# Group statistics by a DRAM round trip and an indirect DMA in place of two small matrix products, in a masked attention kernel

## The chip, the cores and the metric

The kernel runs on one core of one Trainium2 chip. The metric is the device time of one execution in microseconds (us). A core has five engines that work side by side, each through its own list of instructions in order: TensorE (PE in the profile; its weight loads are PEld), VectorE (DVE), ScalarE (ACT), GpSimd (POOL) and SyncE (SP), which here only issues DMAs. GpSimd issues DMAs too. They meet through semaphores.

## The reference

The input x is 32 images of 256 channels and 32 x 32 positions, all float32. Each image is normalised in 32 groups of 8 channels; query, key and value are 1x1 convolutions of the result; eight heads of width 32 attend with a strict causal mask over the 1024 positions; the attention's output is added to x.

```python
def _gn(v, G=32, eps=1e-5):
    g = v.reshape(B_, G, C_ // G, H_, W_)
    m = jnp.mean(g, axis=(2, 3, 4), keepdims=True)
    s = jnp.var(g, axis=(2, 3, 4), keepdims=True)
    return ((g - m) / jnp.sqrt(s + eps)).reshape(v.shape)
...
q = jnp.einsum('oc,bcs->bos', q_w, xf) + q_b[None, :, None]
kv = jnp.einsum('oc,bcs->bos', kv_w, xf) + kv_b[None, :, None]
...
scores = jnp.einsum('bhqd,bhkd->bhqk', q, k) / jnp.sqrt(jnp.asarray(dk, x.dtype))
scores = jnp.where(mask == 0, jnp.asarray(-10000.0, x.dtype), scores)
attn = jnp.where(mask == 0, 0.0, jax.nn.softmax(scores, axis=-1))
out = jnp.einsum('bhqk,bhkd->bhqd', attn, v)
...
x = x + _L0_conv_ref(_gn(x), ...)
```

## The kernel before, in words

**Tiles.** An image lies as 128 partitions x 2 channel groups x 1024 positions. Channels are on partitions, so a group of the normalisation is 8 neighbouring partitions. Heads 0 to 3 belong to the first half of the channels (g = 0), heads 4 to 7 to the second.

**Visits.** The attention of an image is cut into N = 12 visits, six for each g (`VISITS`, lines 583 to 590). A visit computes the transposed scores of four heads for a set of key blocks and queries (`scores`, line 348): a long part of up to 512 columns and a short part, on TensorE's row groups of 32, so that heads 0 and 1 and heads 2 and 3 run beside each other. Scores go to three PSUM tiles of two banks, which every visit uses again; ScalarE takes the exponentials into SBUF (`e`, line 397, twice; `eh`, line 393); on diagonal blocks GpSimd masks them (`mask`, line 329; four of the six visits, `PAIRS`). One visit later TensorE multiplies them by the values (`values`, line 412), and VectorE adds the exponentials of several key blocks together (`add_keys`, line 434), from which the softmax sums are made: folded by accumulating DMAs (`fold`, line 449), stacked (`stack`, line 455), inverted and spread over DRAM. `finish` (line 539) multiplies the attention's numerators by the inverses and adds bias and x: one multiplication (L544), two L547, on VectorE, and a DMA out. It is put two images later: for image b at visits 1, 1, 2 and 4 of image b + 2 (`FINISH`, line 656).

**Normalisation.** `norm_channels` (line 179) takes mean and variance of each channel on VectorE (bn_stats over two halves of 512, then bn_aggr). `norm_mean` (line 187) averages the means over 8 partitions by a small matrix product with the constant `avg` (tile `pm`); ScalarE writes it negated (L195). `norm_deviation` (line 198) makes variance plus squared deviation on VectorE (L205 to L207), `norm_variance` (line 210) averages that by a second product (tile `pv`), ScalarE adds eps (L219). `norm_rstd` (line 221) takes the power -0.5 and the shift on GpSimd (L227, L229). `norm_apply` (line 231) normalises on ScalarE (L244), two instructions for each of four quarters. Then TensorE projects (`project_qk`, `project_v`; `pp` and `ppv`).

**Order.** The order on each engine is written out by hand (`tc.manual_schedule`): every engine issues in the order of the program's text. The main loop (line 750) runs over i, visit v of image b: scores of visit i, what is listed in `at` for i, values of visit i - 1, what is listed in `between`, `add_keys` of visit i - 1, what is listed in `after`. Within a list the order is that of appending; the loop at line 706 appends, image by image, `prepare(b)` and then `finish(b)`, so the `finish` of an older image stands ahead of the `prepare` of a newer one. `PREPARE` (line 652) says at which visit, counted from the image's first, each step of the normalisation is put: -12 and -11 the two channel halves, -9 mean and deviation (in `between`), -8 variance and rstd, -7, -6, -5 and -3 the four quarters of `norm_apply`. Image 1 has its own list (line 705), image 0 is prepared ahead of the loop, with `keep_busy` products meanwhile. `ALIGN` puts 24 drains on VectorE and 64 waits on GpSimd at the start.

## Time and profile before

| | |
|---|---|
| median of 3 runs | 1793.47 us (1793.45 to 1793.51) |
| the profiled execution's own time | 1793.44 us |
| its span in the profile | 1791.7 us |
| mean granted TensorE clock | 0.999 |
| ScalarE waiting for `pm`, for `pv` | 25.9 us in 30 waits, 13.4 us in 30 |
| bn_stats, 512 elements | 679 ns, 128 times |
| bn_aggr, 12 elements | 209 ns, 64 times |
| `pow` on GpSimd (L227) | 716 to 1387 ns, median 1150 |
| `shift` on GpSimd (L229) | 308 to 1619 ns, median 313 |
| SP's DMA of the inverses, 32 KB, issue to landing | 3.2 us |
| GpSimd's DMA of 512 KB, issue to landing | 5.4 to 5.9 us |

How to read it: the span is one execution, and what lies around it is 1.7 us. A row of the timeline gives start and duration in us, engine, source line, operation, and `out<-in` by the program's names; "x2" means that two equal instructions stand merged in one row. What stands in brackets at the end is the engine's idle time ahead of the row and what ended it. TensorE's matrix products overlap, so the durations of one engine's rows can't be added; the distance of their starts can. Image n of 0 to 31 has visits 12n to 12n + 11; image 16's visit 0 starts at 900.21, 1 at 904.78, 2 at 909.33, 3 at 913.53, 4 at 918.56, 5 at 923.16, 6 at 927.79, 7 at 932.36, 8 at 936.92, 9 at 941.12 (first product of the scores), and in it the statistics of image 17 are made.

### The profile page before, as it was taken

Reading aid. Unit: us, or ns where it says so; the run is one execution under the profiler, and the core shown is the slowest. Engines: PE = TensorE matmul, PEld = TensorE weight load, DVE = VectorE, ACT = ScalarE, POOL = GpSimd, SP = SyncE. Lnnn points to the kernel's source line nnn. Section 1 sums busy time; section 2 is a strip of 40 time slices with the busy share of each in tenths; the row PEclk is TensorE's granted clock in tenths of the full one; section 3 lists DMA queues with packets and bytes.
Section 4 is the critical chain, followed back from the end, with each engine's and each line's share of the span. In section 5 each row is a group of like instructions: output and inputs, shape, how many; then the busy total and the mean of one; then the engine's idle time right before and its main releaser. Section 6 shows DMA issues by size and latency. Waiting matters only on the chain.

```text
span 1791.7 us, 81825 instructions
## 1 busy us (share of the span) xinstructions
PE 1784.4 (100%) x37036; PEld 948.2 (53%) x37036; DVE 1673.4 (93%) x1826; ACT 1456.4 (81%) x1990; POOL 881.3 (49%) x903
## 2 busy tenths in 40 slices
PE   9999999999999999999999999999999999999998
PEld 5555555555555555555555555555555555555554
DVE  4689999999999999999999999999999999999998
ACT  6888878888788888788887888878888878888785
POOL 2345544554545555445554455454555544555452
PEclk9999999999999999999999999999999999999999
DMA  2566766767667766766676676767776667666664
GB/s 70 105 115 137 134 134 129 147 135 143 127 126 149 140 138 134 135 139 138 139 135 131 129 150 132 145 125 128 149 141 135 136 134 138 139 139 137 132 107 106
DMA packets 86818, 236.77 MB, mean 132 GB/s; under 512 B 21312, under 2 KB 22336, under 8 KB 70592
## 3 DMA queue, kind: packets, MB, share of 16 engines
q0 software_dynamic: 15872, 97.53, 40.1%
q1 hardware_dynamic: 70448, 133.89, 25.5%
q8 instruction: 290, 4.75, 1.1%
q14 instruction: 64, 0.52, 0.1%
q10 hardware_dynamic: 144, 0.07, 0.0%
HBM read 66.85 MB, written 34.57 MB: 57 GB/s over the span
## 4 chain that ended last, share of the span: by engine, by line
PE 99%; ACT 0%; DVE 0%; issue 0%; POOL 0%; POOLq 0%
PE sT L311 31%; PE acc L422 28%; PE pp L169 26%; PE ppv L169 13%; PE pd L474 1%; PE busy L155 0%; ACT e L397 0%; PE pv L169 0%; PE pm L169 0%; PE wt L148 0%; DVE rb_last L547 0%; ACT eh L393 0%; DVE rb_last L534 0%; DVE turned L531 0%; DVE acc L544 0%
## 5 line engine op out<-in xcount | busy, mean ns | idle before, releaser
L339 POOL TENSOR_SCALAR_AFFINE_SELECT diagonal<-eh 128x512 f32<-128x512 f32 x512 | 632.5, 1256 | 841.5 <-ACT eh L393 840.9
L397 ACT ACTIVATE e<-sT 128x1024 f32<-128x1024 f32 x768 | 744.4, 1022 | 250.3 <-PE sT L311 225.9
L440 DVE TENSOR_TENSOR e<-e,e 128x1024 f32<-128x1024 f32 x314 | 574.2, 1829 | 24.5 <-ACT v L275 3.2
L311 PE MATMUL sT<-q,k 32*64 32x128 f32 (+2 forms) x18432 | 578.4, 372 | 0.1
L311 PEld LDWEIGHTS sT<-q,k 32*64 32x64 f32 x18432 | 394.8, 131 | 188.4 <-PE sT L311 69.6
L169 PE MATMUL pp<-xn,wT 128*32 128x512 f32 x4096 | 492.2, 598 | 0.0
L422 PE MATMUL acc<-e,v 128*32 128x512 f32 (+3 forms) x4608 | 401.0, 450 | 0.0
L393 ACT ACTIVATE eh<-sT 128x768 f32<-128x768 f32 (+1 forms) x384 | 341.7, 890 | 0.0
L422 PEld LDWEIGHTS acc<-e,v 128*32 128x32 f32 x4608 | 149.2, 110 | 261.5 <-issue 238.9
L169 PE MATMUL ppv<-wT,xn 128*32 128x256 f32 x4096 | 247.5, 382 | 0.0
L440 DVE TENSOR_TENSOR diagonal<-diagonal,e 128x1536 f32<-128x1536 f32 x126 | 195.0, 1548 | 16.8 <-PE acc L422 9.2
L169 PEld LDWEIGHTS pp<-xn,wT 128*32 128x32 f32 x4096 | 107.0, 109 | 195.7 <-issue 163.7
L440 DVE TENSOR_TENSOR e<-e,eh 128x1024 f32<-128x1024 f32 x126 | 164.2, 1303 | 6.5
L422 PEld LDWEIGHTS acc<-diagonal,v 128*32 128x32 f32 x4096 | 121.1, 110 | 87.6 <-issue 76.0
L440 DVE TENSOR_TENSOR e<-e,diagonal 128x2048 f32<-128x2048 f32 x63 | 144.2, 2289 | 19.8 <-POOL diagonal L339 19.8
L169 PEld LDWEIGHTS ppv<-wT,xn 128*32 128x32 f32 x4096 | 120.1, 109 | 79.7 <-issue 7.0
L422 PE MATMUL acc<-diagonal,v 128*32 128x128 f32 x4096 | 158.7, 273 | 0.0
L244 ACT ACTIVATE xn<-x,shift,rstd 128x256 f32<-128x256 f32 x248 | 136.8, 608 | 0.6 <-POOL shift L229 0.6
L544 DVE TENSOR_TENSOR num<-num,rb 128x512 f32<-128x512 f32 x124 | 123.3, 994 | 0.2 <-DMA rb<-inverses 0.2
L453 POOL DMA_DIRECT2D e<-e x124 | 103.3, 833 | 38.2 <-issue 38.2
L547 DVE SCALAR_TENSOR_TENSOR rb<-num,v_bias_col,x 128x256 f32<-128x256 f32 x248 | 117.5, 515 | 4.4
L453 POOL DMA_DIRECT2D diagonal<-diagonal x124 | 104.1, 839 | 4.8 <-issue 4.8
(84 smaller groups left out, 984.4 us busy)
## 6 DMA issues: line engine op xcount, KB each, us to landing
x<-in_x_dram SPq DMA_DIRECT2D x124, 256.0 KB, 3.7
diagonal<-diagonal POOLq DMA_DIRECT2D x62, 512.0 KB, 5.4
e<-e POOLq DMA_DIRECT2D x62, 512.0 KB, 5.9
rb<-inverses SPq DMA_DIRECT2D x124, 256.0 KB, 3.9
out_dram<-rb SPq DMA_DIRECT2D x124, 256.0 KB, 4.9
diagonal<-diagonal POOLq DMA_DIRECT2D x62, 256.0 KB, 4.6
folded<-diagonal SPq DMA_DIRECT2D x62, 256.0 KB, 5.1
e<-e POOLq DMA_DIRECT2D x62, 256.0 KB, 5.0
```

The source lines that it names most:

```text
L169: nc.tensor.matmul(out[part], lhsT=lhsT[:, part], rhs=rhs, start=start, stop=stop, skip_group_check=True)
L244: nc.scalar.activation(to, of, AF.Identity, bias=live["shift", b][:, g : g + 1], scale=rstd)
L311: return nc.tensor.matmul(bank[c : c + KEYS, cols], lhsT=live["k", b, g][rows, kb * P + c : kb * P + c + KEYS], rhs=live["q", b, g][rows, ...
L339: nc.gpsimd.affine_select(out=square[:, :, place + s * P : place + (s + 1) * P], in_=raw[:, :, (1 - s) * KEYS : (3 - s) * KEYS], pattern=[ ...
L393: exp = nc.scalar.activation(eh.rearrange("p (n bank) q -> p bank n q", n=2)[:, :, :, :narrow], short[:, :, :, :narrow], AF.Exp)
L397: nc.scalar.activation(e[:, 2 * a : 2 * a + 2, :wide], pairs[a][:, :, :wide], AF.Exp)
L422: nc.tensor.matmul(acc[HD * j : HD * (j + 1), of], lhsT=live["v", b][:, kb, h * HD : (h + 1) * HD], rhs=e[:, j, :], start=first, stop=last ...
L440: nc.vector.tensor_add(to, to, tile_of(b, g, at))
L453: nc.gpsimd.dma_start(out=total[:rows], in_=total[rows : 2 * rows], accum_op=ALU.add)
L474: nc.tensor.matmul(pd[HD * j : HD * (j + 1), of], lhsT=pick, rhs=e[:, j, :], start=start, stop=stop, skip_group_check=True,)
L544: nc.vector.tensor_mul(num, num, rb)
L547: nc.vector.scalar_tensor_tensor(blocks(rb, s), blocks(num, s, (start + s) % 2 == 1), v_bias_col[:, g : g + 1], blocks(xt[:, g, cols], s), ...
```

## The change

For every image but the first, the average over 8 partitions no longer runs on TensorE. `norm_channels` keeps the raw statistics of both halves (24 numbers per channel). `norm_gather` writes them to DRAM by SP; `norm_spread` reads them back by an indirect DMA of GpSimd, row `partition / 8` of an array of 16 rows, so that each partition gets the 8 x 24 numbers of its group; `norm_groups` runs bn_aggr over them, 96 numbers per call. `norm_signs`, on VectorE, makes the negated mean and the variance plus eps, which ScalarE did. `norm_rstd` and `norm_apply` stay as they are.

`PREPARE` is now -12, -11 (channels), -10, -10 (gather, spread), -9 (groups), -8 (signs), -8 (rstd), -7, -6, -5, -3 (apply), all in `after`; the second `norm_channels` is put at the head of its list, ahead of `finish`, the rest is appended. `between` is gone.

In visits 3 and 4 (`SPLIT`) the long part of heads 0 and 1 is issued as 128 and 384 columns, the 128 between the short products of heads 2 and 3. At visits 2 and 8 (`EVEN`) TensorE waits once more for a semaphore count ahead of the values. `ALIGN` becomes 22 drains on VectorE, no waits on GpSimd, 16 drains on SP. The last image is left out of the split, and of the added waits.

```diff
--- before.py
+++ after.py
@@ -89,6 +89,10 @@
     in_range = const.tile([P, ROW], F32, name="in_range")
     nc.gpsimd.memset(in_range, 1.0)
     inv_last = const.tile([P, 4, HALF // HD], F32, name="inv_last")
+    place = const.tile([P, 1], mybir.dt.uint32, name="place")
+    nc.gpsimd.iota(place, pattern=[[0, 1]], base=0, channel_multiplier=1)
+    group_of = const.tile([P, 1], mybir.dt.uint32, name="group_of")
+    nc.vector.tensor_scalar(group_of, place, 3, None, ALU.logical_shift_right)
     eps = const.tile([P, 1], F32, name="eps")
     nc.gpsimd.memset(eps, 1e-5)
 
@@ -179,52 +183,68 @@
         def norm_channels(b, g):
             if g == 0:
                 live["mv", b] = small.tile([P, NG, 2], F32, tag="mv", name=f"mv_{b}")
-            st = small.tile([P, NH, 6], F32, tag="st", name=f"st_{b}_{g}")
+                live["st", b] = small.tile([P, NG, NH * 6], F32, tag="st", bufs=1, name=f"st_{b}")
+            st = live["st", b][:, g, :].rearrange("p (c s) -> p c s", c=NH)
             for c in range(NH):
                 nc.vector.bn_stats(st[:, c, :], live["x", b][:, g, c * HALF : (c + 1) * HALF])
-            nc.vector.bn_aggr(live["mv", b][:, g, :], st)
+            if b == 0:
+                nc.vector.bn_aggr(live["mv", b][:, g, :], st)
+
+        def norm_gather(b):
+
+
+            n = NH * 6
+            each = live["each", b] = dram.tile([P, NG * n], F32, tag="st", name=f"each_{b}")
+            nc.sync.dma_start(out=each, in_=live.pop(("st", b)).rearrange("p g s -> p (g s)"))
+
+        def norm_spread(b):
+
+            n = NH * 6
+            eight = small.tile([P, HALF], F32, tag="turned", bufs=1, name=f"eight_{b}")[:, : CPG * NG * n]
+            live["eight", b] = eight.rearrange("p (c g s) -> p c g s", c=CPG, g=NG)
+            nc.gpsimd.indirect_dma_start(
+                eight, None, live["each", b].rearrange("(m c) s -> m (c s)", c=CPG),
+                bass.IndirectOffsetOnAxis(ap=group_of[:, 0:1], axis=0),
+            )
+
+        def norm_groups(b):
+            for g in range(NG):
+                nc.vector.bn_aggr(live["mv", b][:, g, :], live["eight", b][:, :, g, :])
+
+        def norm_signs(b):
+            mv = live["mv", b]
+            live["minus_mean", b] = small.tile([P, NG], F32, tag="mean", name=f"mean_{b}")
+            nc.vector.tensor_scalar(live["minus_mean", b], mv[:, :, 0], -1.0, None, ALU.mult)
+            live["rstd", b] = small.tile([P, NG], F32, tag="rstd", name=f"rstd_{b}")
+            nc.vector.tensor_scalar(live["rstd", b], mv[:, :, 1], 1e-5, None, ALU.add)
 
         def norm_mean(b):
             mv = live["mv", b]
             pm = misc(f"pm_{b}")
             product(pm[:, :NG], avg, mv[:, :, 0])
-            if b == 0:
-                live["dev", b] = small.tile([P, NG], F32, tag="dev", name=f"dev_{b}")
-                nc.vector.tensor_sub(live["dev", b], mv[:, :, 0], pm[:, :NG])
+            live["dev", b] = small.tile([P, NG], F32, tag="dev", bufs=1, name=f"dev_{b}")
+            nc.vector.tensor_sub(live["dev", b], mv[:, :, 0], pm[:, :NG])
             mean = small.tile([P, NG], F32, tag="mean", name=f"mean_{b}")
             nc.scalar.activation(mean, pm[:, :NG], AF.Identity, scale=-1.0)
             live["minus_mean", b] = mean
 
         def norm_deviation(b):
-            mv, minus_mean = live["mv", b], live["minus_mean", b]
-
-            if b == 0:
-                dev = live["dev", b]
-            else:
-                dev = small.tile([P, NG], F32, tag="dev", name=f"dev_{b}")
-                nc.vector.tensor_add(dev, mv[:, :, 0], minus_mean)
+            mv, dev = live["mv", b], live["dev", b]
             nc.vector.tensor_mul(dev, dev, dev)
             nc.vector.tensor_add(dev, dev, mv[:, :, 1])
-            live["dev", b] = dev
 
         def norm_variance(b):
             pv = misc(f"pv_{b}")
             product(pv[:, :NG], avg, live.pop(("dev", b)))
             rstd = small.tile([P, NG], F32, tag="rstd", name=f"rstd_{b}")
             live["rstd", b] = rstd
-            if b == 0:
-
-                nc.vector.tensor_scalar_add(rstd, pv[:, :NG], 1e-5)
-                return
-            nc.scalar.activation(rstd, pv[:, :NG], AF.Identity, bias=eps)
+            nc.vector.tensor_scalar_add(rstd, pv[:, :NG], 1e-5)
 
         def norm_rstd(b):
             rstd = live["rstd", b]
+            nc.gpsimd.tensor_tensor(rstd, rstd, power, ALU.pow)
             if b == 0:
-
-                nc.gpsimd.tensor_tensor(rstd, rstd, power, ALU.pow)
                 return
-            nc.gpsimd.tensor_tensor(rstd, rstd, power, ALU.pow)
             live["shift", b] = small.tile([P, NG], F32, tag="shift", name=f"shift_{b}")
             nc.gpsimd.tensor_tensor(live["shift", b], live["minus_mean", b], rstd, ALU.mult)
 
@@ -325,6 +345,15 @@
                             if n < len(ops):
                                 done.setdefault((j, c), []).append(score(b, g, bank_of(j), j, ops[n]))
             return done
+
+        def part_of(b, g, bank, entry, of):
+
+            at, _, halves = entry
+            for j in (0, 1):
+                for ((c, kb, first, _, cols),) in halves:
+                    score(b, g, bank[:, j, :], j, (
+                        c, kb, first + of.start, of.stop - of.start, slice(cols.start + of.start, cols.start + of.stop)
+                    ))
 
         def mask(b, g, raw, j):
 
@@ -361,7 +390,9 @@
             long_of = lambda heads, n: scores_of(b, g, lambda j: pairs[j // 2][:, j % 2, :], heads, longs[n : n + 1])
             rest = [lambda: long_of((2, 3), 1)] if len(longs) > 1 else []
             begin = [lambda n=n: long_of((0, 1), n) for n in range(len(longs) - 1, -1, -1)]
-            if i in PAIRS and len(longs) > 1:
+            if b < B - 1 and v in SPLIT:
+                begin = [lambda n=n: part_of(b, g, pairs[0], longs[0], n) for n in (slice(0, P), slice(P, HALF))]
+            if i in PAIRS and len(begin) > 1:
                 first = short_of((2, 3), begin.pop(0), slice(None, None, -1))
             else:
                 first = short_of((2, 3))
@@ -590,6 +621,7 @@
         ]
         N, TOTAL = NG * len(VISITS), 2
         PAIRS = {0: 0, 1: 1, 3: 3, 4: 2}
+        SPLIT = 3, 4
 
         PRODUCTS = [
             (0, [
@@ -629,33 +661,34 @@
             10: [(("L", 4, Q(0, 4)), Q(0, 4)), (("D", 1, Q(0, 4)), Q(0, 4))],
             11: [(("L", 5, Q(0, 3)), Q(1, 4)), (("L", 5, Q(3, 4)), Q(3, 4)), (("H", 5, Q(0, 2)), Q(2, 4))],
         }
-        at, between, after = {}, {}, {}
+        at, after = {}, {}
 
         def when(i, f, where=at):
             where.setdefault(i, []).append(f)
 
         def prepare(b, whens):
             for n, f in zip(whens, [
-                lambda: norm_channels(b, 0), lambda: norm_channels(b, 1), lambda: norm_mean(b),
-                lambda: norm_deviation(b), lambda: norm_variance(b), lambda: norm_rstd(b),
+                lambda: norm_channels(b, 0), lambda: norm_channels(b, 1), lambda: norm_gather(b), lambda: norm_spread(b),
+                lambda: norm_groups(b), lambda: norm_signs(b), lambda: norm_rstd(b),
             ] + [lambda hf=hf, g=g: norm_apply(b, hf, g) for hf in range(NH) for g in range(NG)]):
                 if n is None:
                     f()
                 elif isinstance(n, tuple):
-                    when(n[0], f, between)
+                    n[1].setdefault(n[0], []).insert(0, f)
                 else:
                     when(n, f, after)
 
 
 
         PROJECT = (-5, -4, -3, -2, -1, 0, 1, 2, 3, 4, 5, 6)
-        PREPARE = (-12, -11, -9, -9, -8, -8, -7, -6, -5, -3)
+        PREPARE = (-12, -11, -10, -10, -9, -8, -8, -7, -6, -5, -3)
         SUMS = (3, 7, 10, 13)
         LOAD = 7
         SPREAD = (2, 2, 4, 5)
         FINISH = (N + 13, N + 13, N + 14, N + 16)
         every = range(4)
-        ALIGN = 24, 64
+        EVEN = 2, 8
+        ALIGN = 22, 0, 16
 
         with tc.manual_schedule(engines={ENG.PE, ENG.Activation, ENG.DVE, ENG.Pool, ENG.SP}):
 
@@ -683,6 +716,8 @@
                 nc.scalar.sem_inc(live["arrived"], 1)
                 nc.sync.wait_ge(live["arrived"], 2)
                 load(1)
+            for _ in range(ALIGN[2]):
+                nc.sync.drain()
             norm_deviation(0)
             norm_variance(0)
             turn_weights(0)
@@ -702,7 +737,7 @@
                 else:
                     when(n, f)
             if B > 1:
-                prepare(1, (None, None, 0, 1, 2, 2, 3, 4, 5, 7))
+                prepare(1, (None, None, None, None, 1, 2, 2, 3, 4, 5, 7))
             for b in range(B):
                 first, last = b * N, b == B - 1
                 if b >= 1:
@@ -715,7 +750,9 @@
                         if n % NH == 0:
                             when(v, lambda n=n: with_scores(n // NH))
                         when(v, lambda b=b, n=n, cols=cols: load_part(b, n // NH, cols))
-                    prepare(b, [(first + n,) if k in (2, 3) else first + n for k, n in enumerate(PREPARE)])
+                    prepare(b, [
+                        (first + n, after) if k == 1 else first + n for k, n in enumerate(PREPARE)
+                    ])
                 if not last:
                     for n in every:
                         v = first + SUMS[n]
@@ -757,9 +794,9 @@
 
                     sums(3, SUMMED[v], False)
                 if i:
+                    for _ in range(EVEN.count((i - 1) % N) if i < B * N - N else 0):
+                        nc.tensor.wait_ge(bank_free, live["free"])
                     values(b, v)
-                    for f in between.pop(i, ()):
-                        f()
                     if b < B - 1 or v not in SUMMED or v == 1:
                         add_keys(b, v)
                 if i in (B * N - 2, B * N - 1):
@@ -767,7 +804,7 @@
                     sums(3, SUMMED[v])
                 for f in after.pop(i, ()):
                     f()
-            assert not at and not between and not after
+            assert not at and not after
             inside = end_last(B - 1)
         for p in reversed(pools):
             p.release()
```

## Prediction

> **What bounds the kernel now.** I read the page first, then the waits, then the timeline of one image (image 16 of 0 to 31) engine by engine; the page says who sets the pace, the waits who is nearly late, the timeline by how much.

> ```profile
> span 1791.7 us, 81825 instructions
> PE 1784.4 (100%) x37036; PEld 948.2 (53%) x37036; DVE 1673.4 (93%) x1826; ACT 1456.4 (81%) x1990; POOL 881.3 (49%) x903
> PE 99%; ACT 0%; DVE 0%; issue 0%; POOL 0%; POOLq 0%
> ```

> TensorE is never without work, and the chain that ended last is TensorE for 99%. The starts of its matmuls repeat from image to image within 2 ns, 55.09 us per image of twelve visits: it waits for nobody. So a change can win only what TensorE no longer issues, and loses whatever makes TensorE wait. VectorE, at 93%, is the engine to watch. The waits name one edge of the normalisation that just closes:

> ```profile
> ACT xn L244 <- POOL shift L229: 0.6, 2, 0.3
> ```

> ScalarE waited for `shift` in two images only, 0.3 us each. How close is it in the others? VectorE, in order, around the statistics for image 17 (columns: start, duration, engine, line, operation):

> ```profile
> 908.89 0.99 DVE L440 TENSOR_TENSOR e<-e 128x512 f32<-128x512 f32 x1
> ...
> 920.12 0.15 DVE L205 TENSOR_TENSOR dev<-mv,mean 128x2 f32<-128x2 f32 x1
> ...
> 923.07 2.60 DVE L440 TENSOR_TENSOR e<-e,e 128x2048 f32<-128x2048 f32 x1
> 925.60 1.11 DVE L544 TENSOR_TENSOR num<-num,rb 128x512 f32<-128x512 f32 x1
> 926.75 0.88 DVE L547 SCALAR_TENSOR_TENSOR rb<-num,v_bias_col,x 128x256 f32<-128x256 f32 x2
> 927.54 2.28 DVE L440 TENSOR_TENSOR e<-e,diagonal 128x2048 f32<-128x2048 f32 x1
> 929.93 4.40 DVE L440 TENSOR_TENSOR e<-e,e 128x2048 f32<-128x2048 f32 x2
> ```

> GpSimd and ScalarE at the same time:

> ```profile
> 926.14 1.15 POOL L227 TENSOR_TENSOR rstd<-rstd,power 128x2 f32<-128x2 f32 x1
> 927.37 0.31 POOL L229 TENSOR_TENSOR shift<-mean,rstd 128x2 f32<-128x2 f32 x1
> ```

> ```profile
> 927.72 1.09 ACT L244 ACTIVATE xn<-x,shift,rstd 128x256 f32<-128x256 f32 x2
> 928.98 1.94 ACT L397 ACTIVATE e<-sT 128x1024 f32<-128x1024 f32 x2 [0.17 <-PE sT L311]
> ```

> The reader is to see three things. VectorE has no gap from 908.89 to 932: what is put behind `finish` of visit 4 (L544, L547) starts at 927.6, though TensorE ended that visit at 923.16. `shift` ends at 927.68 and ScalarE's `xn` starts at 927.72: no slack. And the exponentials follow `xn` on ScalarE, 0.17 us after they could.

> [...] in images 0 and 1

> ```profile
> 32.65 1.39 POOL L227 TENSOR_TENSOR rstd<-rstd,power 128x2 f32<-128x2 f32 x1 [4.31 <-ACT rstd L219]
> 34.11 0.75 POOL L229 TENSOR_TENSOR shift<-mean,rstd 128x2 f32<-128x2 f32 x1
> ```

> ```profile
> 99.67 1.62 POOL L229 TENSOR_TENSOR shift<-mean,rstd 128x2 f32<-128x2 f32 x1
> ```

> The free durations are 0.72 (`pow`) and 0.31 (`shift`). The first `pow` ended 0.55 after a VectorE addition of two tiles ended at 33.48; both `shift`s ended 0.05 after one (34.81 and 101.23). [...] the orders above are the program's. [...] here the small 32 KB `inverses` takes 3.2 from issue to landing, which I use.

> **The change part by part.** Per image, times of image 16.

> *TensorE, products removed.* The visit with `pm` (913.53 to 918.56) takes 5.025, the equal visit without it (941.12 to 946.11) 4.989: 0.036. The one with `pv` takes 4.606 against 4.552, of which 0.010 is another projection: 0.044. Together 0.080; the products hide most of the turn from values to scores.

> *The split.* Visit 0 of each image already has the opening that visits 3 and 4 of the first group get (64, long 128, 128, long 384): there the closing pair of short products starts 0.941 after the first score, in visit 3 at 0.963. So 0.022 less for each of two visits, 0.044; bounds 0.044 less and 0.032 more (visit 0 as a whole is 0.016 longer, which I put down to its second, split long product).

> *Waits before values at visits 2 and 8.* The semaphore has been waited for inside the same scores: nothing[...]. If not hidden, some 0.04 each (half of a 0.087 pair of waits on GpSimd at the start).

> *ScalarE* loses `mean` (0.17) and `rstd` (0.26), both ahead of idle time of 0.75 or more: nothing.

> *Gather and spread.* The two bn_stats, put ahead of `finish` 0 and 1, end at about 911.2 instead of 914.6. SP issues the gather behind the `folded` transfer (911.0, 0.51), at 911.6; it lands by 914.8. GpSimd then issues the indirect transfer, past nothing but its own idle time (its next work, the mask, starts at 917.46 and has 3 us before values read it). No indirect transfer is in this trace: 0.8 (a direct one) to 3 us on GpSimd; landing 3.2 to 5.9 (small one, large one on the same queue). I take 1 and 4: 919.8. Groups come at about 922.3 on VectorE, 2.5 later. At the long ends they would wait 1.4 us.

> *VectorE.* Gone are two bn_aggr (0.24 with their gap) and `dev` (920.20 to 920.68: 0.47). The first aggr is ahead of 908.89, an addition held by a TensorE wait that ends just then, so its removal gives nothing. New are two bn_aggr over 96 elements instead of 12: 0.21 each if length doesn't matter, 1.67 if all of it does; at the 1.3 ns per element of bn_stats (679 for 512) 0.32, 0.70 for both with gaps. Sum: 0.70 - 0.24 - 0.47 = 0. `finish` of visit 4 still ends at 927.6.

> *Signs, the step that decides.* They are appended to the list of visit 4, behind that `finish`; before, no VectorE work fed `pow`, which waited for the mask ahead of it. Two small operations, 0.16 each and overlapping, end at 927.8. The addition of 2048 columns follows at once (927.7 to 930.0); `pow` gets its signal some 0.08 later, [...] and ends 0.55 behind the addition, at 930.5. The next addition has started 0.1 behind the first (930.1 to 932.4), so `shift` ends at 932.4 and `xn` starts at 932.5 instead of 927.72: **4.75 late**. Queued behind `xn` on ScalarE are the exponentials of visits 6, 7 and 8; their score banks are what TensorE's next visits write. Slack on that way: 0.17 ahead of the exponentials of visit 6, 0.30 ahead of `num` (932.50), and at most 0.06 where visit 9 starts 0.16 behind the last exponential of visit 8. So TensorE stops for 4.75 - 0.5 = 4.25 us, spread over the starts of visits 7 to 9. VectorE is held at 908.89 by TensorE again in the next image, so the lag comes back each time; and what TensorE saves in visits 3 and 4 is swallowed, since the late end hangs on visit 1.

> *How often.* `finish` of visit 4 exists in images 2 to 30: 29 times.

> *The start.* 64 waits of GpSimd hold the second mask of `avg` until 7.15, and the first `pm` (7.61) follows it; without them `pm` can follow the warm-up products at 7.42: 0.19 gained. The new iota and shift lie ahead of the first x (3.56), hidden. Drains on SP: nothing waits there.

> Sum against the profiled execution (1793.44, median 1793.47): 1793.44 + 29 x 4.25 - 0.19 - 2 x 0.12 = **1916**.

> **The rivals.**
> *Faster: the chain stays off the path.* TensorE then keeps 31 x 0.080 + 31 x 0.044 + 0.19 = 4.0: 1789.4. It holds if `shift` ends by 928.2 (slack 0.5), so if the signs end by 927.0 and find no addition running. For it: two images took a wait of 0.3 with TensorE unmoved. Against it: the order of VectorE's list, and no gap since 908.89 to catch up in.
> [...] as once in image 1 (98.87, 0.72 long, addition from 98.94): `shift` alone is blocked, 2.3 late, TensorE 1.8: 1845. Without any blocking 1.25 late, 0.7: 1814.
> *The indirect transfer is later still, or bn_aggr dearer:* each us at the groups adds one us per image; 1.4 more gives 1956.

> **How the numbers follow.** Both blocked 0.46 (own range 1895 to 1940); one or none blocked 0.17; later still 0.08; off the path 0.29, because I could misjudge how far VectorE lags. Of this last, 0.17 ends below 1789.9 and 0.12 above: a difference of 0.2% (3.6 us) is about what a measurement can tell from none. The range 1788.5 to 1940 leaves out the latest case and a sliver below. Faster 0.17, same 0.12, slower 0.71.

> **What would show it.** Right: ScalarE's `xn` waits for `shift`, 29 times, some 4.7 us; `pow` about 2.7 long, `shift` 1.9; TensorE idle at the starts of visits 7 to 9. Wrong: `shift` ending within 5 us of the start of visit 5, or `finish` of visit 4 ending well ahead of 4.4 us behind it. With TensorE's scores at 1.38 in visits 3 and 4 the split is as reckoned; groups waiting for the DMA would show the transfer mis-sized.

## The result and the profile after

| | before | after |
|---|---|---|
| median | 1793.49 us (1793.45 to 1793.88, 6 runs) | 1914.79 us (1909.08 to 1919.12, 6 runs) |
| ratio, with its 95% interval | | 1.0675 [1.0658, 1.0692] |
| the profiled execution's own time, its span | 1793.44, 1791.7 | 1919.12, 1917.4 |
| mean granted TensorE clock | 0.999 | 0.978 |
| one image, first score to first score, images 2 to 30 | 55.09 | 59.36 |

The kernel is slower by 121 us in the medians, and 29 images x (59.36 - 55.09) = 124 of the 126 us between the two profiled executions lie in the images with a `finish` two images back. The page first:

```profile
span 1917.4 us, 81783 instructions
PE 1842.4 (96%) x37036; PEld 947.8 (49%) x37036; DVE 1645.2 (86%) x1796; ACT 1440.0 (75%) x1928; POOL 847.6 (44%) x935
PE 65%; DVE 19%; POOL 7%; ACT 4%; issue 3%; DMA 1%; DVEq 0%; SPq 0%; ACTq 0%
```

The chain that ended last was TensorE for 99%; now it runs through VectorE, GpSimd and ScalarE too. No engine's busy share has grown; the chain passes from one to another, which is what a new wait looks like. The waits (total us, times, longest) name it, on ScalarE and then on TensorE:

```profile
ACT xn L264 <- POOL shift L249: 130.9, 30, 5.2
```

```profile
PE sT L331 <- ACT e L428: 64.3, 58, 2.6
```

The first was 0.6 us in 2 waits. Image 16, in order: VectorE, GpSimd, ScalarE, TensorE. Visit 5 starts at 983.90, 6 at 988.53, 7 at 995.02.

```profile
986.55 0.68 DVE L575 TENSOR_TENSOR num<-num,rb 128x512 f32<-128x512 f32 x1
987.26 0.88 DVE L578 SCALAR_TENSOR_TENSOR rb<-num,v_bias_col,x 128x256 f32<-128x256 f32 x2
988.06 0.16 DVE L217 TENSOR_SCALAR mean<-mv 128x2 f32<-128x2 f32 x1
988.13 0.16 DVE L219 TENSOR_SCALAR rstd<-mv 128x2 f32<-128x2 f32 x1
988.20 2.29 DVE L471 TENSOR_TENSOR e<-e,diagonal 128x2048 f32<-128x2048 f32 x1
990.59 4.15 DVE L471 TENSOR_TENSOR e<-e,e 128x2048 f32<-128x2048 f32 x2
```

```profile
988.38 2.70 POOL L245 TENSOR_TENSOR rstd<-rstd,power 128x2 f32<-128x2 f32 x1 [3.90 <-DVE rstd L219]
991.16 1.78 POOL L249 TENSOR_TENSOR shift<-mean,rstd 128x2 f32<-128x2 f32 x1
```

```profile
987.81 0.70 ACT L278 ACTIVATE q<-pp,qk_bias 128x512 f32<-128x512 f32 x1
992.97 1.09 ACT L264 ACTIVATE xn<-x,shift,rstd 128x256 f32<-128x256 f32 x2 [4.46 <-POOL shift L249]
993.97 1.91 ACT L428 ACTIVATE e<-sT 128x1024 f32<-128x1024 f32 x2
```

```profile
992.55 0.61 PE L453 MATMUL acc<-eh,v 128*32 128x256 f32 x8
995.02 0.56 PE L331 MATMUL sT<-q,k 32*64 32x128 f32 x16 [1.86 <-ACT e L428]
995.93 1.79 PE L331 MATMUL sT<-q,k 32*64 32x512 f32 x32 [0.35 <-ACT e L428]
```

The signs stand behind `finish` (L575, L578), and the 2048-column addition starts 0.07 us behind the start of the second. `pow` (L245) begins 0.18 after that addition, takes 2.70 instead of 0.72 and ends 0.59 after it; `shift` (L249) ends 0.05 after the first half of the next row's two additions. ScalarE has been idle for 4.46 us; its exponentials are late, and TensorE, which needs their score banks, stops at the start of visit 7 and again inside it.

That is 3.28 us of the 4.38 that an image loses: the nine images of 2 to 30 in which the clock stays whole take 58.26, and 54.98 is what they take when nothing waits (the first experiment). (The profile shows 2.2 of the 3.28 as idle time; the rest lies between the products of visit 7: its first projection, `pp`, starts 2.63 behind its first score, where the kernel before had 1.40.) The other 1.10 is TensorE's clock. In 20 of the 29 images it is halved (granted 0.50) for one stretch of 3.413 us or two. Image 15 (columns: stretch, its length, each engine's busy time and instructions, granted clock, DMA share, GB/s):

```profile
931.00:936.54 5.54, 3.33 (x58) 1.43 (x50) 5.19 (x5) 2.97 (x5) 3.30 (x3) 1.00 0.33 50
936.54:939.95 3.41, 3.41 (x36) 1.62 (x40) 3.31 (x5) 3.41 (x6) 1.76 (x4) 0.50 0.94 229
939.95:946.00 6.05, 6.05 (x100) 2.62 (x96) 3.87 (x7) 5.49 (x9) 2.81 (x4) 1.00 0.69 105
```

TensorE was busy for 3.33 of the 5.54 us ahead, then at half clock for one stretch. Image 15 took 59.41, image 16 without such a stretch 58.29. The spread of the new kernel's runs goes with it: over 10 us, with clocks from 0.978 (1919 us) to 0.985 (1909), where those of the kernel before agree within 0.5.

### The profile page after: what moved, and what is told of

Same layout as the page of the kernel before. It is cut to its first block, busy times and chain, and to the rows that moved or that the text cites. A ratio compares the mean times of both kernels' runs of the same rounds, so it can differ in the third digit from the quotient of the medians.

```text
span 1917.4 us, 81783 instructions
## 1 busy us (share of the span) xinstructions
PE 1842.4 (96%) x37036; PEld 947.8 (49%) x37036; DVE 1645.2 (86%) x1796; ACT 1440.0 (75%) x1928; POOL 847.6 (44%) x935
## 3 DMA queue, kind: packets, MB, share of 16 engines
q8 instruction: 290, 4.75, 1.1%
## 4 chain that ended last, share of the span: by engine, by line
PE 65%; DVE 19%; POOL 7%; ACT 4%; issue 3%; DMA 1%; DVEq 0%; SPq 0%; ACTq 0%
PE sT L331 20%; PE pp L173 20%; PE acc L453 17%; DVE e L471 8%; PE ppv L173 7%; DVE diagonal L471 4%; POOL rstd L245 4%; DVE rb L578 3%; ACT e L428 3%; POOL shift L249 3%; DVE num L575 2%; DVE mv L212 1%; ACT xn L264 1%; DMA each<-st 1%; PE pd L505 1%
## 5 line engine op out<-in xcount | busy, mean ns | idle before, releaser
L428 ACT ACTIVATE e<-sT 128x1024 f32<-128x1024 f32 x768 | 745.3, 1024 | 303.2 <-PE sT L331 303.2
L368 POOL TENSOR_SCALAR_AFFINE_SELECT diagonal<-eh 128x512 f32<-128x512 f32 x512 | 466.1, 931 | 681.5 <-ACT eh L424 681.2
L331 PE MATMUL sT<-q,k 32*64 32x64 f32 (+1 forms) x18928 | 613.1, 372 | 64.5 <-ACT e L428 64.3
L471 DVE TENSOR_TENSOR e<-e,e 128x1024 f32<-128x1024 f32 x314 | 542.4, 1727 | 51.7 <-ACT v L295 21.0
L331 PEld LDWEIGHTS sT<-q,k 32*64 32x64 f32 x18928 | 407.8, 132 | 285.7 <-ACT e L428 82.6
L173 PE MATMUL pp<-xn,wT 128*32 128x512 f32 x4096 | 516.3, 622 | 0.0
L471 DVE TENSOR_TENSOR diagonal<-diagonal,e 128x1536 f32<-128x1536 f32 x126 | 187.8, 1490 | 17.9 <-issue 6.2
L471 DVE TENSOR_TENSOR e<-e,eh 128x1024 f32<-128x1024 f32 x126 | 193.4, 1535 | 6.4
L471 DVE TENSOR_TENSOR e<-e 128x512 f32<-128x512 f32 x64 | 57.2, 894 | 132.8 <-PE acc L453 98.4
L245 POOL TENSOR_TENSOR rstd<-rstd,power 128x2 f32<-128x2 f32 x32 | 80.5, 2515 | 111.1 <-DVE rstd L219 104.3
L205 POOL DMA_INDIRECT eight<-each,group_of x31 | 41.6, 1342 | 192.5 <-DMA each<-st 192.5
L578 DVE SCALAR_TENSOR_TENSOR rb<-num,v_bias_col,x 128x256 f32<-128x256 f32 x248 | 121.6, 531 | 4.4
```

The lines of the kernel that those rows point to most:

```text
L173: nc.tensor.matmul(out[part], lhsT=lhsT[:, part], rhs=rhs, start=start, stop=stop, skip_group_check=True)
L205: nc.gpsimd.indirect_dma_start(eight, None, live["each", b].rearrange("(m c) s -> m (c s)", c=CPG), bass.IndirectOffsetOnAxis(ap=group_of[ ...
L245: nc.gpsimd.tensor_tensor(rstd, rstd, power, ALU.pow)
L331: return nc.tensor.matmul(bank[c : c + KEYS, cols], lhsT=live["k", b, g][rows, kb * P + c : kb * P + c + KEYS], rhs=live["q", b, g][rows, ...
L368: nc.gpsimd.affine_select(out=square[:, :, place + s * P : place + (s + 1) * P], in_=raw[:, :, (1 - s) * KEYS : (3 - s) * KEYS], pattern=[ ...
L428: nc.scalar.activation(e[:, 2 * a : 2 * a + 2, :wide], pairs[a][:, :, :wide], AF.Exp)
```

## Experiments

**The theories.** Theory: the signs' place in VectorE's list makes `pow` and `shift` start under a VectorE addition of 2048 columns, and they end only behind it (by 0.59 and 0.05 us, above); `xn` comes late, and TensorE waits for the exponentials behind it. That is called the hold here; the expectations call it the lock, or being shut out, and no more is meant than those times. Rivals: the DMA round trip or the longer bn_aggr makes the loss; or the lateness of the signs does it without a hold; or the split of the products costs.

**signs_ahead**: after, with the signs (step 5 of the list) put at the head of visit 4's list.

```diff
-                        (first + n, after) if k == 1 else first + n for k, n in enumerate(PREPARE)
+                        (first + n, after) if k in (1, 5) else first + n for k, n in enumerate(PREPARE)
```

> The changed kernel with the signs at the head of visit 4's list, ahead of finish, nothing else moved. Theory (signs queued behind finish, then pow and shift each shut out by an addition of 2048 columns): the signs are ready before the mask of visit 4 releases GpSimd, shift ends 4.2 to 4.7 us after the start of visit 5, ScalarE's xn waits under 0.5 us, TensorE doesn't stop; per image 0.111 us less than before in visits 3 and 4, so 1793.5 - 31 x 0.111 + 0.2 at the start = 1790.2 us. Rival (the round trip over DRAM, with GpSimd and VectorE waiting for it, is what costs): stays over 1850.

Measured: 1792.39 us (1791.22 to 1794.09), ratio to the kernel before 0.999 [0.9983, 0.9997]. VectorE and GpSimd in image 16:

```profile
924.18 0.15 DVE L217 TENSOR_SCALAR mean<-mv 128x2 f32<-128x2 f32 x1
924.25 0.15 DVE L219 TENSOR_SCALAR rstd<-mv 128x2 f32<-128x2 f32 x1
924.32 0.68 DVE L575 TENSOR_TENSOR num<-num,rb 128x512 f32<-128x512 f32 x1
925.03 0.88 DVE L578 SCALAR_TENSOR_TENSOR rb<-num,v_bias_col,x 128x256 f32<-128x256 f32 x2
925.83 2.28 DVE L471 TENSOR_TENSOR e<-e,diagonal 128x2048 f32<-128x2048 f32 x1
```

```profile
924.49 1.10 POOL L245 TENSOR_TENSOR rstd<-rstd,power 128x2 f32<-128x2 f32 x1 [2.38 <-DVE rstd L219]
925.67 0.29 POOL L249 TENSOR_TENSOR shift<-mean,rstd 128x2 f32<-128x2 f32 x1
```

The same two instructions now stand ahead of L575. `pow` meets the multiplication of 512 columns and ends 0.59 after it; `shift` meets the second L578 and ends 0.05 after that, held for 0.1 us only. All the loss is gone with the round trip, the two long bn_aggr and the split in place: the images take 54.98, with no wait of TensorE. So none of those makes it. Against the expectation 2.2 us are missing, of which 1.97 stand at the end (from the last three rows of products, `pc`, to the end: 7.25 us instead of 5.28).

**late_pow_only**: before, with one tiny VectorE instruction behind `finish` that `pow` has to wait for. Nothing else of the change.

```diff
             rstd = live["rstd", b]
...
+            nc.vector.tensor_scalar(rstd, rstd, 1.0, None, ALU.mult)
             nc.gpsimd.tensor_tensor(rstd, rstd, power, ALU.pow)
```

> The kernel before, with its matrix products and no DMA for the statistics, and one VectorE multiplication by 1.0 of rstd ahead of pow, issued behind finish of visit 4. Theory: this alone gives pow 2.7 us, shift 1.8 us, xn some 4.4 us late, and about 1913 us (1905 to 1925, TensorE's clock dropping in about two images of three). Rival (the DMA path costs): 1793.5.

Measured: 1939.55 us (1938.63 to 1941.51), ratio 1.0813 [1.0797, 1.083]. VectorE and GpSimd in image 16:

```profile
994.88 0.16 DVE L227 TENSOR_SCALAR rstd<-rstd 128x2 f32<-128x2 f32 x1
994.95 2.28 DVE L441 TENSOR_TENSOR e<-e,diagonal 128x2048 f32<-128x2048 f32 x1
```

```profile
995.12 2.69 POOL L228 TENSOR_TENSOR rstd<-rstd,power 128x2 f32<-128x2 f32 x1 [1.62 <-DVE rstd L227]
997.89 1.72 POOL L230 TENSOR_TENSOR shift<-mean,rstd 128x2 f32<-128x2 f32 x1
```

The same two blocked operations from one added instruction: the place suffices. It costs more than the whole change mostly because TensorE's clock was halved in 27 of 29 images instead of 20 (mean granted clock 0.970 and 0.978); the two with a whole clock lose 58.48 - 55.09 = 3.39 us, about as after (3.28).

**vector_waits_for_shift**: after, with a VectorE instruction that reads `shift` and so holds the addition back until GpSimd is done. The signs stay behind `finish`: late, but with no addition beside GpSimd.

```diff
             nc.gpsimd.tensor_tensor(live["shift", b], live["minus_mean", b], rstd, ALU.mult)
+            nc.vector.tensor_scalar(live["shift", b], live["shift", b], 1.0, None, ALU.mult)
```

> The changed kernel with one VectorE multiplication by 1.0 of shift behind the signs, so that VectorE stands still while GpSimd makes pow and shift and no addition can shut them out. The signs stay late. Theory with the shut-out as the larger part: pow 0.72 and shift 0.31 us, shift ready 1.5 us after xn could start instead of 4.45, TensorE loses under 1 us per image: 1791 to 1820 us, although VectorE stands still for 1.3 us per image. Rival (lateness behind finish alone, GpSimd's durations being no matter): 1900 or more.

Measured: 1800.26 us (1798.35 to 1803.27), ratio 1.0038 [1.0024, 1.0051]. GpSimd in image 16:

```profile
928.31 0.73 POOL L245 TENSOR_TENSOR rstd<-rstd,power 128x2 f32<-128x2 f32 x1 [3.90 <-DVE rstd L219]
929.12 0.19 POOL L249 TENSOR_TENSOR shift<-mean,rstd 128x2 f32<-128x2 f32 x1
```

Signs late and `pow` late, but `pow` is 0.73 and `shift` 0.19 long, which is what they take with nothing on VectorE beside them. In the median `xn` comes 1.28 after its place in signs_ahead (4.59 in after), and 114 of the 121 us are gone. So of 4.59 us of lateness the place alone makes 1.28 (the added instruction is in it), the hold the rest. The images of this trace differ in how late `xn` is, and so show what is free: 1.27 late costs visit 7 nothing, 1.46 costs it 0.18, 1.88 costs 0.61, 2.67 costs 1.38. That is the lateness less 1.28 each time.

**xn_late_by_one, xn_late_by_four**: signs_ahead, with one or four ScalarE passes over 1024 columns ahead of the first `xn`. They make `xn` late with no hold and nothing on GpSimd.

```diff
                 live["xn", b, hf] = work.tile([P, NG, HALF], F32, tag="xn", bufs=3, name=f"xn_{b}_{hf}")
+                for _ in range(4 if b > 1 and hf == 0 else 0):
+                    nc.scalar.activation(live["xn", b, hf], live["x", b][:, :, :HALF], AF.Identity)
```

> signs_ahead with one more ScalarE pass over 1024 columns of x (some 1.1 us, estimated from the 0.97 of an exponential over 1024 columns) ahead of the first xn of every image from 2 on; xn overwrites what it writes. It delays ScalarE's xn and what is queued behind it as a late shift does, without a lock and without GpSimd. Theory after the result (slack on the way xn, exponentials, scores is 1.1 to 1.2 us: 4.45 late gave 3.29 of stall): no stall or hardly any, 1792 to 1797. Rival (the prediction's slack of 0.5): 30 x 0.6 = 18 us more, 1810.

> The same with four such passes, some 4.4 us, about what the blocked pow and shift gave in the kernel after (4.45). Theory (the lateness of xn alone sets TensorE's loss; the lock only makes it late): 30 x 3.2 = 97 us of waits, and up to 33 us more where the stall halves TensorE's clock for one window of 3.4 us: 1885 to 1925, with the stall at the start of visit 7, released by the exponentials. Rival (part of the loss in the kernel after comes from the lock or from VectorE itself, not by way of xn): clearly less, 1860 or below.

Measured: one pass 1792.49 us (1791.62 to 1793.98), ratio 0.9991 [0.9983, 0.9999]; four passes 1903.74 (1901.2 to 1904.52), 1.0606 [1.0592, 1.062]. ScalarE and TensorE with four, image 16:

```profile
982.26 4.35 ACT L256 ACTIVATE xn<-x 128x1024 f32<-128x1024 f32 x4
986.70 1.09 ACT L266 ACTIVATE xn<-x,shift,rstd 128x256 f32<-128x256 f32 x2
```

```profile
988.76 0.56 PE L333 MATMUL sT<-q,k 32*64 32x128 f32 x16 [1.71 <-ACT e L430]
989.67 1.79 PE L333 MATMUL sT<-q,k 32*64 32x512 f32 x32 [0.35 <-ACT e L430]
```

The pattern on TensorE is that of after, row for row. `xn` 1.17 us late costs nothing, 4.45 late costs 3.17 us per image where the clock stays whole. Both fit the rule of vector_waits_for_shift, lateness less 1.28, and so do after (4.59 late, 3.31 lost in image 16) and late_pow_only (4.67 and 3.39). So lateness of `xn` accounts for all of TensorE's wait. The 11 us between this kernel and after are mostly clock: halved in 11 of 29 images here, in 20 there (mean granted clock 0.988 and 0.978).

**signs_ahead_channels_behind**: signs_ahead with the second `norm_channels` at the end of its list, so that the round trip starts later: 2.8 us in the median of the images, where 3.4 were expected.

```diff
-                        (first + n, after) if k in (1, 5) else first + n for k, n in enumerate(PREPARE)
+                        (first + n, after) if k == 5 else first + n for k, n in enumerate(PREPARE)
```

> signs_ahead with the second norm_channels at the end of its list again, behind finish 0 and 1, instead of at the head: the round trip through DRAM starts some 3.4 us later. The margin at the groups is 0.4 us in the kernel after, so VectorE waits some 3.0 us for the indirect transfer in each of 30 images. Theory (VectorE has no gap to catch up in, and what is behind the groups comes late): TensorE loses between 1 and 2.7 us per image, 1820 to 1870. Rival (the half visit does not matter, since a late shift has over a microsecond of slack and VectorE regains the rest): 1792 to 1797, with VectorE waiting at the groups all the same.

Measured: 1796.06 us (1794.68 to 1801.34), ratio 1.0017 [1.0008, 1.0025]. A miss of the theory: the rival's range held. The margin that it started from was wrong as well: in after and in signs_ahead the groups start 1.7 to 1.8 us behind the landing of the transfer in the median, not 0.4.

```profile
DVE mv L212 <- DMA eight<-each,group_of: 18.4, 16, 2.2
```

VectorE waits for the transfer in 16 instructions, at most 2.2 us, and regains it: its waits for `acc` fall from 27.1 to 19.6 us, those for the mask from 17.1 to 12.4. The half visit is worth some 3.7 us in all.

**split_only**: before, with the split of visits 3 and 4 and nothing else (diff: the hunks of `part_of`, `SPLIT` and `begin` above).

> The kernel before with the split of the long part in visits 3 and 4 and nothing else. From the changed kernel's trace the scores of these visits take 1.387 instead of 1.403 us: 62 x 0.016 = 1.0 us less, 1792.5 us. Rival (the prediction's upper bound, a visit like visit 0 as a whole): 1794.5 us.

Measured: 1799.13 us (1797.22 to 1800.82), ratio 1.0027 [1.0017, 1.0036]: a miss, by 6.6 us and on the other side. Visits 3 and 4 became shorter (5.025 to 5.010, 4.606 to 4.583), but in ten images TensorE stops for 0.07 to 1.24 us at other places. In image 3:

```profile
188.64 1.45 PE L311 MATMUL sT<-q,k 32*64 32x128 f32 x43
191.02 0.33 PE L311 MATMUL sT<-q,k 32*64 32x64 f32 x5 [0.93 <-issue]
```

The products wait for nothing that the profile shows ("issue"). Each such stop in this trace begins 1.3 to 2.3 us behind the start of a DMA packet of 16 KB on the instruction queue q8. A packet holds some 256 instructions of TensorE: in the kernel before 74153 weight loads, products and waits come in 290 packets, here 992 more in 294. One starts about every 6 us (6.1 in the median of before). (Smaller stops of 0.15 to 0.19 us in visit 7 of images 3, 18 and 25 are the hold again: behind a stop of over a microsecond in visit 1, `shift` met an addition and took 1.99.) The kernel before has 2306 TensorE instructions per image, 9 x 256 + 2, and the transfers hardly move: in each of images 2 to 30 nine start, the ninth 52.1 to 53.6 us behind the image's first score. The split makes them 2338. The kernel after has 2306 again: what the products of `pm` and `pv` took out, the split and the two added waits put back.

**signs_ahead_32_waits**: more waits, no other work.

```diff
-        EVEN = 2, 8
+        EVEN = (2, 8) + tuple(range(12)) * 2 + tuple(range(0, 12, 3)) * 2
```

> signs_ahead with 32 more waits per image on TensorE ahead of the values (three or so more at every visit, all for a count already reached): no arithmetic added, none removed. TensorE then has 2338 instructions per image in the records, as split_only has, instead of 2306. Theory (what matters is the number of TensorE instructions modulo the 256 of one 16 KB instruction transfer, since 2306 = 9 x 256 + 2 lets the transfers stand still in the image while 2338 lets them wander over all its places): scattered stalls of 0.1 to 1.2 us come back in a third of the images, as in split_only, some 5 to 10 us in all: 1797 to 1802. Rival (the split itself made the stalls of split_only, by the order of its products): 1792.4, as signs_ahead. Second rival (a wait costs TensorE 0.04 us each): 31 x 32 x 0.04 = 40 us more, evenly in every image: 1832.

Measured: 1796.11 us (1792.72 to 1800.39), ratio 1.0013 [1.0006, 1.0019], so 3.7 us slower than signs_ahead. Two waits in a row became one instruction, so the count is 2322. In the profiled run 24 of 29 images take 54.98 as before: a wait for a count already reached costs nothing that shows. Five stop for 0.13 to 0.94 us, all in visit 10; each stop begins 2.0 to 2.4 us behind the start of a q8 transfer. The direction is the theory's; the count of images is lower than expected.

**no_split_short_count, no_split_padded_count**: signs_ahead_padded_tail (below) with `SPLIT = ()`; the second with 68 waits per image instead of 2 (66 more; the expectation says 64), which restore 2306.

> signs_ahead_padded_tail without the split of visits 3 and 4. TensorE loses 32 instructions per image, 2274 instead of 2306, which is 30 short of nine transfers of 256. Theory (the number of instructions decides where in the image a transfer falls): the split's 0.111 us per image is lost, 3.4 us in all, which alone would give 1793.9, and scattered stalls behind instruction transfers come on top, 3 to 10 us: 1797 to 1804. Rival (stalls come with the split or with the added waits): 1793.9 and no stalls.

> The same without the split, with 64 more waits per image on TensorE ahead of the values, at every visit; two waits in a row make one instruction, so the 2306 instructions per image are restored. Theory: no stalls, each image the same, 1793.9: the kernel with more instructions is the faster of the two by 3 to 10 us. Rival (waits are no help or cost something): as no_split_short_count or above.

Measured: 1800.46 us (1794.24 to 1806.32), ratio 1.0031 [1.002, 1.0042], with 2274 instructions; 1805.05 (1802.13 to 1806.97), 1.006 [1.0047, 1.0074], with 2306. The second is a miss of the theory as I had put it: the count was restored and the stops grew. (The 0.111 in the expectation was split and removed products together; undisturbed images take 55.01 in both, so the split is worth 0.032.) TensorE in image 27 of the second:

```profile
1560.48 1.03 PE L453 MATMUL acc<-e,v 128*32 128x512 f32 x7
1562.49 0.83 PE L453 MATMUL acc<-e,v 128*32 128x512 f32 x8 [0.97 <-issue]
```

The first product that is late is the image's 947th in image 6, the 944th in 11, 938th in 17, 931st in 23, 928th in 27, 924th in 29, from the start of visit 10 back into visit 9: about two instructions (a weight load and a product) earlier per image, which is the 2 in 9 x 256 + 2. The count only says how fast the transfers wander; what matters is which instructions they meet. In the kernel before and after they meet harmless ones, here those of visit 9. That is inferred: no run moved a transfer alone.

Not all that these two kernels lose is of this kind. In the trace of the first, 2.8 us are the end, where GpSimd stood still for 4.09 us although it has the 30 drains (see the next experiment), and 1.7 are the hold, in image 1. And in both, visit 4 loses 0.25 to 0.62 us in 14 images (5.4 us together), always at the same scores. There TensorE waits for a semaphore that its own scores just ahead raise, and in these images it is raised later, 1.3 to 1.5 us behind the start of GpSimd's indirect transfer, which is late in them. Why the two go together was not tested. With the split no such stop is seen, though the transfer is as late in images 16 and 30 of signs_ahead_padded_tail.

**signs_ahead_padded_tail, signs_ahead_late_index**: signs_ahead with 30 drains on GpSimd ahead of the end; the second also with the iota and the shift moved behind the normalisation of image 0.

```diff
+            for _ in range(30):
+                nc.gpsimd.drain()
             inside = end_last(B - 1)
```

> signs_ahead with 30 drains on GpSimd put ahead of the end, where GpSimd is idle for 7 us, so that it has as many instructions as in the kernel before (1232 in the records instead of 1202). Theory (GpSimd fetches one more 8 KB block of instructions behind the last branch, because its stream is 30 shorter and the end straddles a block): the time from the last visit's products to the end falls from 7.25 back to 5.3 us, total 1790.4. Rival (the longer tail comes from elsewhere, for instance SyncE's 16 drains or the code's length as a whole): 1792.4, as signs_ahead.

> signs_ahead with the same 30 drains on GpSimd, and with the iota and the shift that make the index moved behind the normalisation of image 0. Theory (VectorE's shift stands between the bn_aggr and the first average and holds TensorE's first average for 0.2 us): the first scores come at 16.0 instead of 16.2 us, and the total is 0.2 below that of signs_ahead_padded_tail, 1790.2 if the tail is mended too. Rival (the start hangs on the waits that GpSimd lost, as the prediction had it, or on the drains): the first scores stay at 16.2.

Measured: 1790.52 us (1789.63 to 1792.65), ratio 0.9982 [0.9975, 0.999]; 1790.38, 0.9984 [0.9977, 0.9991]. The tail is 5.30 us again, as expected: behind the last branch GpSimd stood still for 2.84 us between a drain and its next instruction in signs_ahead, for 0.92 in the kernel before, and one more 8 KB packet of instructions was fetched. That the packet is the cause is not shown: it starts when the standstill is over. In 13 of the 14 traces the tail goes with the number of GpSimd's instructions (5.3 us with 1232 or 1233, 7.1 to 7.6 with 1201 or 1202), but no_split_short_count, with 1232, has 8.1. So the drains mend this kernel's end, and what makes GpSimd stand still stays open. Moving the index changed nothing in the time, and the first scores came at 16.72, not at 16.0: that theory of the start falls. signs_ahead_padded_tail is the version that beats both kernels, by some 3 us and by 124 us.

## Why the prediction was right, step by step

- **Products removed**, 0.080 per image: measured 0.079 (5.025 and 4.606 against 4.989 and 4.563 without the split).
- **Split**, 0.044: measured 0.032, within its bounds. The waits at visits 2 and 8 cost nothing, as said. What I didn't see is that both also bear on where TensorE's instruction transfers fall; alone, the split costs 5 us.
- **Gather and spread.** SP issued the gather 2.2 us after visit 2 began (2.3 predicted), but it took 5.7 us to release GpSimd, not 3.2. The indirect transfer then held GpSimd for 1.55 us and landed 3.1 us behind its start, not 1 + 4. The two errors nearly cancel: the groups started 1.8 us behind the landing, 2.5 predicted. In image 16 of after, with the landings of all 31 (counted from the start of the issue):

```profile
978.02 1.55 POOL L205 DMA_INDIRECT eight<-each,group_of  x1 [6.00 <-DMA each<-st]
```

```profile
982.96 1.02 DVE L212 BATCH_NORM_AGGREGATE mv<-eight 128x2 f32<-128x96 f32 x2
```

```profile
DMA to landing us min/median/max: 2.6/3.0/4.9
```

- **bn_aggr over 96 elements**, 0.70 for both: 1.02. VectorE took it without loss: `finish` of visit 4 ended 4.24 after the start of visit 5, predicted 4.44.
- **Signs.** They ended 4.39 after the start of visit 5 (4.6 predicted); `pow` 2.70 long (2.7), `shift` 1.78 (1.9), `xn` 4.52 later than before (4.75). The ends behind the additions, 0.55 and 0.05 as read in the trace of before, came out as 0.59 and 0.05. A VectorE operation that starts while a GpSimd one runs was not held (last section). One reading was off: 0.31 is not the free time of `shift`, which is 0.19; in the kernel before it ends 0.05 behind the second L547, which holds it as well.
- **Slack, the term that was mis-sized.** "Slack 0.5" was summed from ScalarE's idle gaps. It had to be read at the consumer: the first exponential of visit 6 ended at 930.00, and visit 7 started at 932.36, 2.36 later. In after it starts 0.05 behind that exponential, so 2.31 were free there. The exponential ended 4.23 later than before; 4.23 - 2.31 = 1.92 should be lost at the start of visit 7, and visit 6 is 1.92 longer. The other 1.39 is inside visit 7: 1.23 in its scores, which wait bank by bank for an engine that is behind, 0.16 in the projections behind them. The tightest place is there: 1.28 are free against signs_ahead (vector_waits_for_shift), and so 1.2 against the kernel before, not 0.5.
- **The place of the stall.** Predicted over the starts of visits 7 to 9; it is at the start of visit 7 and within it, and visits 8 and 9 keep their 4.20 and 4.99.
- **4.25 us per image** came out as 4.38 against 54.98, or 4.27 against 55.09, but not by its own working: 3.28 of waiting, 1.0 less than reckoned (0.7 by the slack, the rest by `xn`), and 1.10 of halved clock, which the prediction didn't have. Over 29 images that is 28 us too many and 32 missing. The two errors cancel, so it is luck that 1916 came so near; the sign, the mechanism and the order of size are not.
- **The start**, -0.19: not to be told from scatter. The first average came at 7.61 to 7.83 in three traces with the start of before and at 7.13 to 7.82 in those with the start of after, and the scores 8.38 to 8.40 behind it in most of both.
- **The end**, 1.9 us in after: not in the prediction.
- The rival "off the path", 1789.4, is what the change gives with the signs ahead: 1790.5 with the tail mended.

## What to carry to other kernels

A step that moves from one engine to another takes its place in that engine's list; ask what VectorE runs at the moment it hands over to GpSimd (under an addition `pow` took 2.70 us instead of 0.72), not only whether the engine has time. Slack is read where the late result is consumed, and a stall of TensorE is to be priced with the clock that it may cost (here 1.10 us per image beside 3.28 of waiting). When a kernel has no wait at all, a few instructions more or fewer can cost microseconds, whatever they do (here 16 more per image in signs_ahead_32_waits 3.7 us, 32 in split_only 5), and restoring their number need not bring these back (no_split_padded_count, with 2306, lost 11): look for stops that nothing in the profile releases.
